# One PSUM bank for y and for the side work, a third bank for A dt, and side work that is begun only where it can end: a state-space layer with a feed-forward block on one NeuronCore

## The chip, the cores and the metric

The kernel runs on one core of a Trainium2 chip. The metric is the device time of one execution in microseconds. All arithmetic is in float32.

## The reference

Two layers follow each other on x of 2 sequences of 1024 tokens with 512 channels. The first is a selective state-space layer with N = 128 states per channel, the second a feed-forward block with 2048 hidden units. Each adds its result to its input and normalises it.

```python
xn = x * rsqrt(mean(x * x) + 1e-6) * norm_w
xn = xn * sigmoid((xn @ select_proj_w.T + select_proj_b) * select_gate)
delta, B, C = split(xn @ x_proj_w.T)                 # 128 columns each
delta = softplus(delta @ dt_proj_w.T + dt_proj_b)    # 512 channels
A = -exp(A_log)                                      # 512 x 128
for t in range(1024):
    h = exp(delta[t][:, None] * A) * h + (delta[t] * xn[t])[:, None] * B[t][None, :]
    y[t] = (h * C[t][None, :]).sum(-1)
x = layernorm(x + (y + x * D_param) @ out_proj_w.T)
x = layernorm(x + (silu(x @ w_gate.T) * (x @ w_up.T)) @ w_down.T)
```

## The kernel before

**Stages, halves and steps.** The 2048 tokens are cut into 64 stages of 32 tokens (`st`). A stage has two halves (`h = 2 * st + i`), and a half has eight steps (`r = k % 8`), so the main loop runs over `k` from 0 to 1023. A step covers 32 groups of channels for the 128 states: `[128 states, 32, 32 tokens]`, 1024 elements per partition.

**One step.** TensorE makes two matmuls of `bu` (dt x B, line 692) into one of two `bu` tiles of two PSUM banks each, and, between them, two matmuls of `a` (A dt, `decay_mm`, line 404) for the step after. Each `a` tile is one bank, from the pool `ps_a`, which has two. ScalarE takes the exponential of each `a` bank (`decay_exp`, line 411) into `a_sb`, which has three places. VectorE adds the state carried over from the stage before into the first token (line 705) and runs the scan `h = a * h + bu` along the tokens (line 708). GpSimd spreads dt and dt x over diagonal tiles (`diag`: `ddt`, line 375, and `du`, line 385), which the matmuls take as their moving operand.

**y.** `y_round(h, b)` is four 256-column matmuls that contract h with C for four tokens; a half needs eight rounds, and they read the half before. `ROUNDS` says at which of the eight steps they are issued: three after step 1, three after step 4, two after step 7. The two halves of a stage share one tile of the pool `ps_y`, a PSUM bank of its own. Once both are done, `y_out` (line 430) copies the bank to SBUF on ScalarE, and GpSimd picks the wanted elements and adds them up. Every fourth stage this adds a `post` generator: the transposes `zT`, the output projection `op`, the first norm.

**The side work.** All else is in generators that a small class, `Work`, advances between the steps: `pre` (the projections of the next lot of 256 tokens: `ss`, `sel`, `xp`, `b`, `z`, `uT`, `t0`), `post`, and `ffn` (`x1T`, gate and up `gu`, down `d`; its weights are streamed, four pieces of 512 KB ahead). A generator yields "E" where other engines' work follows, "P" where it wants to begin a run of matmuls in a PSUM bank, and "H" between the pieces of such a run. Only one run is under way at a time, since all of it uses a single bank (`ps_m`, tag "m", one buffer); the next run's first matmul waits until the last reader of the bank is done. `work.others()` runs at the start of each step and advances all generators that stand at "E". `work.tensor()` issues one piece after a step's matmuls. How many is set by `PARTS` and a running credit:

```python
credit = min(credit + PARTS[r], 6)
for _ in range(min(credit, 4) if PARTS[r] else 0):
    if not work.tensor():
        break
    credit -= 1
```

So a run may stand half done over a step that belongs to y. `work.finish` forces a lot's `pre` to its end before the stage that needs it. After the last scan the rest of the side work is run with six banks.

The order of the instructions of each engine is the order in which the program issues them. PSUM's eight banks are: two `bu` tiles (4), `a` (2), side work (1), y (1).

Of the kernel before, what the change touches and what calls it, by code (L numbers as in the profile page):

```python
# [9 lines left out]
FP = mybir.dt.float32  # L10
AF = mybir.ActivationFunctionType
ALU = mybir.AluOpType
# [3 lines left out]
P = 128  # L16
# [3 lines left out]

ROUNDS = ((), (0, 1, 2), (), (), (3, 4, 5), (), (), (6, 7))
PARTS = (4, 0, 3, 3, 0, 3, 3, 0)
RMS_EPS = 1e-6
# [11 lines left out]
def kernel(  # L35
# [17 lines left out]
    nc = tc.nc  # L53
# [67 lines left out]
    half_pool = tc.alloc_tile_pool(name="half", bufs=2)  # L121
    ps_y = tc.alloc_tile_pool(name="ps_y", bufs=1, space=PSUM)
    ps_m = tc.alloc_tile_pool(name="ps_m", bufs=1, space=PSUM)
# [34 lines left out]
    def misc(name):  # L158
        return bank_pool[0].tile([P, 512], FP, tag="m", name=name)
# [5 lines left out]
    def pre(c):  # L165
# [32 lines left out]
        for m in range(NM):  # L198
            nc.scalar.activation(xT[:, m, :], xT[:, m, :], AF.Copy, scale=col(V_NORM, m))
        yield "P"  # L200
        ps = misc(f"ss_{c}")
# [11 lines left out]
        for a in (slice(0, 2), slice(2, 4)):  # L213
# [3 lines left out]
            yield "E"  # L217
        yield "P"


        for m in range(NM):
            ps = misc(f"sel_{c}_{m}")
            yield from matmuls(ps, sel_w, m, xn)
            nc.scalar.activation(
                u[:, m, :], ps[:, 0:n], AF.Relu,
                bias=neg[:, 1, m : m + 1], scale=neg[:, 0, m : m + 1],
            )
            nc.scalar.activation(
                dt[:, m, :], ps[:, 0:n], AF.Abs, bias=gate_b[:, m : m + 1], scale=col(V_GATE, m)
            )  # L230
            yield "P" if m + 1 < NM else "E"
# [6 lines left out]
        yield "P"  # L238


        for g, dst in ((0, low), (2, c_sb)):
            ps = misc(f"xp_{c}_{g}")
            yield from matmuls(ps, xp_w, g, xn)
            nc.scalar.copy(dst, ps[:, 0:n])
            yield "P"

# [10 lines left out]
        for st in range(n_s):  # L257
# [4 lines left out]
            )  # L262
        yield "P"

        for a in range(0, NM, 2):
            ps = misc(f"z_{c}_{a}")
            for m in (a, a + 1):
                nc.tensor.matmul(  # L268
                    ps[:, ts(m - a, n)], dt_w[:, ts(m, P)], low, start=True, stop=True
                )  # L270
                yield "H" if m == a else "E"
            for m in (a, a + 1):
                z = ps[:, ts(m - a, n)]
                nc.scalar.activation(u[:, m, :], z, AF.Relu, bias=col(V_DTB, m))
                nc.scalar.activation(dt[:, m, :], z, AF.Abs, bias=col(V_DTB, m))
            yield "P" if a == 0 else "E"
        yield from softplus(dt, u)
# [4 lines left out]
        for j in range(n_j):  # L282
            yield "P"
            ps = misc(f"uT_{c}_{j}")
# [15 lines left out]
            if c == 0:  # L300
                load(0)
                diag(0, 0)
                diag(0, 1)
        yield "P"
        ps = misc(f"t0_{c}")
# [42 lines left out]
    def carry_a(st):  # L348

        if st % NSB == 0:  # L350
            return
        cd = carried[st]
        nc.gpsimd.tensor_tensor(cd, a_n, cd, ALU.mult)
        nc.scalar.activation(cd, cd, AF.Exp, scale=-1.0)

# [59 lines left out]
    def y_round(h, b):  # L415


        st, i = divmod(h, 2)
        if i == 0 and b == 0:
            ys[st] = ps_y.tile([P, 512], FP, tag="y", name=f"y_{st}")  # L420
        at = 28 + 28 * b
        for m in range(NM):
            nc.tensor.matmul(  # L423
                ys[st][ts(m, 32), ts(i, 256)], cz[st % 3][:, at : at + 32],
                hs[h][:, ts(m, 64), ts(b, 4)],
                start=(i == 0 and b == 0), stop=(i == 1 and b == 7),
                skip_group_check=True,
            )

    def y_out(st):  # L430

        tt, s = divmod(st, 4)
        if s == 0:
            yrs[tt] = post_pool.tile([P, 4, P], FP, tag="yr", name=f"yr_{tt}")
        yc = post_pool.tile([P, P, 4], FP, tag="yc", name=f"yc_{st}")
        nc.scalar.copy(yc, ys.pop(st).rearrange("p (q t) -> p q t", t=4))  # L436
        nc.gpsimd.tensor_tensor(yc, yc, pick.unsqueeze(1).to_broadcast([P, P, 4]), ALU.mult)  # L437
        nc.gpsimd.tensor_tensor(yc[:, :, 0:2], yc[:, :, 0:2], yc[:, :, 2:4], ALU.add)
        nc.gpsimd.tensor_tensor(yrs[tt][:, s, :], yc[:, :, 0], yc[:, :, 1], ALU.add)
        if s == 3:  # L440
            work.add(post(tt), front=True)
# [3 lines left out]
    def post(tt):  # L445
# [6 lines left out]
        yield "E"  # L452
        yield "P"
        ps = misc(f"zT_{tt}")
# [10 lines left out]
        nc.sync.dma_start(x1, xf[tt])  # L465
        yield "P"
        ps = misc(f"op_{tt}")
# [22 lines left out]
    def ffn(tt, row):  # L490
# [24 lines left out]
        x1T = ffn_pool.tile([P, NM, P], FP, tag="x1T", name=f"x1T_{tt}")  # L515
        yield "P"
        ps = misc(f"x1T_{tt}")
# [7 lines left out]
        for what in order:  # L525
            part = int(what[1])
            if what[0] == "g":
# [3 lines left out]
                for f in range(0, NH, 2):  # L531
                    fetch(at + 4)
                    yield "P"
                    ps = misc(f"gu_{tt}_{part}_{f}")
# [20 lines left out]
            for half in range(2):  # L555
                fetch(at + 4)
                yield "P"
                ps = misc(f"d_{tt}_{part}_{half}")
# [48 lines left out]
    class Work:  # L607


        def __init__(self):  # L610
            self.gens, self.holder = [], None

# [17 lines left out]

        def tensor(self):

            if self.holder is not None:
                if self.holder[1] != "H":
                    return False
                self.step(self.holder)
                return True
            for item in self.gens:
                if item[1] == "P":
                    self.holder = item  # L640
                    self.step(item)
                    return True
            return False

        def finish(self, item):
# [21 lines left out]
    pres, begun, credit = {}, set(), 0  # L667
    for k in range(NG):
        h, m, pair = place(k)
        st, i = divmod(h, 2)  # L670
        r = k % 8
        work.others()
        if r == 0:
            hs[h] = half_pool.tile([P, 256, S], FP, tag="h", name=f"h_{h}")

            if i == 1 and st:
                y_out(st - 1)
            if i == 0:
# [58 lines left out]
    y_out(NS - 1)  # L737
    ps_a.release()
# [8 lines left out]

    for pool in (bank_pool[0], ps_m, ps_y, hid_pool[0], ffn_pool, post_pool, main):
        pool.release()
# [67 lines left out]
```

## Time and profile before

| | |
|---|---|
| time, three runs | 2867.26, 2872.88, 2875.75 us (median 2872.88) |
| the profiled execution | 2875.05 us, span 2873.2 us |
| mean granted TensorE clock | 0.985 |
| TensorE matmuls busy | 2751.4 us, 96% |
| VectorE busy | 2532.2 us, 88%; of it the scans 1024 x 2.287 us |
| ScalarE busy | 1561.8 us, 54%; of it the exponentials of A dt 2048 x 0.585 us |
| GpSimd busy | 1783.0 us, 62% |
| first scan begins, last scan ends | at 42.5 us, at 2785.2 us |

The profile gives each group of instructions by the line of the kernel, the engine, and "out<-in" with the names of the tiles. In the timeline the first column is the start in microseconds from the span's start, the second the length, and brackets hold the idle time before it and what ended it. A float32 matmul shows as two rows, and rows overlap where matmuls run in different parts of the array or are still draining: so a matmul's cost is read from the start of one group to the start of the next.

### The profile page before, as it was taken

What the parts mean: (1) busy time and instruction counts of PE and PEld (TensorE: products, weight loads), DVE (VectorE), ACT (ScalarE), POOL (GpSimd) and SP (SyncE); (2) the same over time, 40 slices, a digit from 0 to 9 for tenths busy, and PEclk for the clock granted to TensorE, in tenths of its full rate; (3) what the DMA queues carried; (4) which work ended last, traced back from release to release, by engine and by line L of the source; (5) the groups of instructions that cost most, each with busy time, mean ns of one, the idle gap of its engine ahead of it and who ended that gap; (6) DMA issues with size and microseconds to landing.
All of it is one profiled execution on the core that took longest, in us unless ns stands there. A gap on an engine that the chain in (4) does not pass through costs nothing.

```text
span 2873.2 us, 57382 instructions
## 1 busy us (share of the span) xinstructions
PE 2751.4 (96%) x22728; PEld 1496.3 (52%) x22728; DVE 2532.2 (88%) x2176; ACT 1561.8 (54%) x3105; POOL 1783.0 (62%) x2016
## 2 busy tenths in 40 slices
PE   7879899999999999999999999999999999999998
PEld 4324455555555555455555555555555555555558
DVE  3999799899998999999999999999999999999970
ACT  4545555555565556645555555555556555555543
POOL 4556665666666666666567667566665666666643
PEclk6999999999999999999999999999999999999999
DMA  2011221324213231222312233122321322333236
GB/s 74 16 30 65 78 87 61 105 66 133 85 53 112 89 107 62 82 98 89 111 51 88 97 103 109 56 84 92 114 96 51 115 96 91 114 101 100 98 112 230
DMA packets 112379, 258.66 MB, mean 90 GB/s; under 512 B 11568, under 2 KB 49456, under 8 KB 112112
## 3 DMA queue, kind: packets, MB, share of 16 engines
q1 hardware_dynamic: 112112, 254.99, 27.4%
q8 instruction: 181, 2.97, 0.4%
q14 instruction: 86, 0.70, 0.1%
HBM read 242.23 MB, written 12.71 MB: 89 GB/s over the span
## 4 chain that ended last, share of the span: by engine, by line
PE 75%; DVE 18%; issue 3%; ACT 2%; POOL 1%; DMA 0%; SPq 0%; DVEq 0%; POOLq 0%; ACTq 0%
PE bu L692 27%; PE gu L539 17%; DVE h L708 16%; PE y L423 13%; PE d L561 6%; PE a L404 5%; PE sel L186 2%; PE op L470 1%; PE xp L186 1%; DVE bu L705 1%; ACT a_sb L411 1%; PE b L250 1%; PE ss L203 0%; PE z L268 0%; DMA ub_d<-uT 0%
## 5 line engine op out<-in xcount | busy, mean ns | idle before, releaser
L708 DVE TENSOR_TENSOR_SCAN h<-a_sb,bu 128x1024 f32<-128x1024 f32 x1024 | 2341.2, 2287 | 160.7 <-PE bu L692 46.3
L411 ACT ACTIVATE a_sb<-a 128x496 f32<-128x496 f32 x2048 | 1089.0, 585 | 1078.5 <-PE a L404 957.1
L404 PE MATMUL a<-ddt,a_t 32*128 32x512 f32 x4096 | 1253.9, 647 | 3.0 <-ACT t L314 2.8
L692 PE MATMUL bu<-du,ub 32*128 32x512 f32 x4096 | 1210.5, 647 | 47.9 <-DVE h L708 27.3
L375 POOL TENSOR_TENSOR ddt<-dt,hot 128x512 f32<-128x512 f32 x512 | 532.6, 1048 | 310.2 <-PE a L404 310.2
L539 PEld LDWEIGHTS gu<-x1T,w 128*128 128x128 f32 x4096 | 482.2, 192 | 230.9 <-issue 181.3
L385 POOL TENSOR_TENSOR du<-ub,hot 128x512 f32<-128x512 f32 x512 | 535.0, 1049 | 48.9 <-PE a L404 44.9
L539 PE MATMUL gu<-x1T,w 128*128 128x128 f32 x4096 | 537.1, 283 | 11.7 <-DVE x L474 4.0
L692 PEld LDWEIGHTS bu<-du,ub 32*128 32x128 f32 x4096 | 342.9, 185 | 376.9 <-issue 206.8
L423 PE MATMUL y<-h,cz 128*32 128x256 f32 x8192 | 527.3, 386 | 1.3 <-DVE h L708 1.3
L423 PEld LDWEIGHTS y<-h,cz 128*32 128x32 f32 x8192 | 228.2, 110 | 407.8 <-issue 296.4
L404 PEld LDWEIGHTS a<-ddt,a_t 32*128 32x128 f32 x4096 | 379.4, 185 | 31.3 <-ACT a_sb L411 19.9
L579 POOL TENSOR_SCALAR gu<-gu 128x256 f32<-128x256 f32 x128 | 108.3, 846 | 309.6 <-ACT gu L547 309.3
L705 DVE TENSOR_TENSOR bu<-bu,cd 128x32 f32<-128x32 f32 x992 | 185.6, 187 | 98.2 <-PE a L404 92.0
L561 PE MATMUL d<-w,hid 128*128 128x256 f32 x1024 | 256.7, 393 | 12.6 <-ACT t L314 4.4
L561 PEld LDWEIGHTS d<-w,hid 128*128 128x128 f32 x1024 | 183.9, 190 | 131.7 <-issue 86.1
L437 POOL TENSOR_TENSOR yc<-yc,pick 128x512 f32<-128x512 f32 x64 | 66.5, 1039 | 151.1 <-ACT yc L436 151.0
L362 POOL TENSOR_TENSOR cd<-cd,h 128x256 f32<-128x256 f32 x124 | 106.4, 858 | 45.5 <-DVE h L708 45.5
L587 POOL TENSOR_TENSOR hid<-gu,e 128x256 f32<-128x256 f32 x128 | 93.0, 727 | 62.1 <-ACT e L585 60.2
L547 ACT COPY gu<-gu 128x512 f32<-128x512 f32 x128 | 75.1, 587 | 63.2 <-PE gu L539 63.1
L580 POOL TENSOR_TENSOR gu<-gu 128x256 f32<-128x256 f32 x128 | 94.2, 736 | 10.7
L567 DVE TENSOR_TENSOR x<-x,d 128x256 f32<-128x256 f32 x64 | 25.6, 399 | 72.3 <-PE d L561 72.3
(86 smaller groups left out, 1272.1 us busy)
## 6 DMA issues: line engine op xcount, KB each, us to landing
w<-in_wgu_s_dram SPq DMA_DIRECT2D x256, 512.0 KB, 3.6
w<-in_wd_s_dram SPq DMA_DIRECT2D x128, 512.0 KB, 3.6
cd<-dt_d SPq DMA_DIRECT2D x62, 256.0 KB, 3.9
ub<-ub_d SPq DMA_DIRECT2D x64, 128.0 KB, 2.0
ub_d<-bt SPq DMA_DIRECT2D x64, 64.0 KB, 1.8
ub_d<-uT SPq DMA_DIRECT2D x64, 64.0 KB, 1.8
zT<-in_x_q_dram SPq DMA_DIRECT2D x16, 256.0 KB, 4.1
x<-in_x_dram SPq DMA_DIRECT2D x16, 256.0 KB, 3.8
```

The source lines that it names most:

```text
L362: nc.gpsimd.tensor_tensor(cd, cd, last, ALU.mult)
L375: nc.gpsimd.tensor_tensor(ddts[j][:, m, :, :], made[lot_of[st]][0][:, a + m, toks(st)].unsqueeze(1).to_broadcast([P, 16, S]), hot[:, ts(i, ...
L385: nc.gpsimd.tensor_tensor(dus[j][:, m, :, :], uv[:, a + m, :].unsqueeze(2).to_broadcast([P, 16, S]), hot.unsqueeze(1).to_broadcast([P, 16, ...
L404: nc.tensor.matmul(ps, a_t[ts(g, 32), m, :], ddts[k // 4][ts(g, 32), m % 2, :, :], start=True, stop=True,)
L411: nc.scalar.activation(a_sb[:, k % 3, ts(b, 16), 1:], ps[:, :, 1:], AF.Exp, scale=-1.0)
L423: nc.tensor.matmul(ys[st][ts(m, 32), ts(i, 256)], cz[st % 3][:, at : at + 32], hs[h][:, ts(m, 64), ts(b, 4)], start=(i == 0 and b == 0), s ...
L539: nc.tensor.matmul(ps[:, ts(2 * a + b, P)], w[:, a, k, :], x1T[:, k, :], start=(k == 0), stop=(k == NM - 1),)
L561: nc.tensor.matmul(ps[:, 0:HD], hid[:, f, :], w[:, f % 4, :], start=(f == 0), stop=(f == NH - 1),)
L579: nc.gpsimd.tensor_scalar_max(g, g, -80.0)
L692: nc.tensor.matmul(bu[:, ts(b, 16), :], prepared[st][ts(g, 32), 1, :], dus[k // 4][ts(g, 32), m % 2, :, :], start=True, stop=True,)
L705: nc.vector.tensor_tensor(first, first, left[:, at : at + 2, i, :], ALU.add)
L708: nc.vector.tensor_tensor_scan(hs[h][:, ts(r, 32), :].rearrange("p q t -> p (q t)"), a_sb[:, k % 3, :, :].rearrange("p q t -> p (q t)"), b ...
```

## The change

- The pool `ps_y` goes. y of a half (no longer of a stage) is a tile of the side work's bank, and `y_out` is called for each half, at the start of step 4.
- The eight rounds are issued in two runs of four, after steps 2 and 3. Ahead of the first, `work.idle()` ends whatever run of side work is open.
- The freed bank becomes a third buffer of `ps_a`.
- A generator yields the number of pieces of a run where it yielded "P", and `work.tensor(room)` begins a run only if that number fits into `ROOM` at this step. `PARTS` changes, and the credit is gone.
- The exponential of the carried decay is issued at the end of step 7, not with its product at step 5.

```diff
-ROUNDS = ((), (0, 1, 2), (), (), (3, 4, 5), (), (), (6, 7))
-PARTS = (4, 0, 3, 3, 0, 3, 3, 0)
+ROUNDS = ((), (), (0, 1, 2, 3), (4, 5, 6, 7), (), (), (), ())
+PARTS = (4, 4, 0, 0, 3, 3, 4, 4)
+
+ROOM = (8, 4, 0, 0, 8, 4, 4, 8)
...
-    ps_y = tc.alloc_tile_pool(name="ps_y", bufs=1, space=PSUM)
...
         nc.gpsimd.tensor_tensor(cd, a_n, cd, ALU.mult)
-        nc.scalar.activation(cd, cd, AF.Exp, scale=-1.0)
+
+    def carry_exp(st):
+        if st % NSB:
+            nc.scalar.activation(carried[st], carried[st], AF.Exp, scale=-1.0)
...
     def y_round(h, b):
...
-        st, i = divmod(h, 2)
-        if i == 0 and b == 0:
-            ys[st] = ps_y.tile([P, 512], FP, tag="y", name=f"y_{st}")
+        if b == 0:
+            ys[h] = misc(f"y_{h}")
...
-    def y_out(st):
-
+    def y_out(h):
+
+        st, i = divmod(h, 2)
...
-        yc = post_pool.tile([P, P, 4], FP, tag="yc", name=f"yc_{st}")
-        nc.scalar.copy(yc, ys.pop(st).rearrange("p (q t) -> p q t", t=4))
-        nc.gpsimd.tensor_tensor(yc, yc, pick.unsqueeze(1).to_broadcast([P, P, 4]), ALU.mult)
+        yc = post_pool.tile([P, 64, 4], FP, tag="yc", name=f"yc_{h}", bufs=2)
+        nc.scalar.copy(yc, ys.pop(h)[:, 0:256].rearrange("p (q t) -> p q t", t=4))
+        nc.gpsimd.tensor_tensor(yc, yc, pick.unsqueeze(1).to_broadcast([P, 64, 4]), ALU.mult)
...
-        def tensor(self):
+        def tensor(self, room=64):
 
             if self.holder is not None:
                 if self.holder[1] != "H":
                     return False
+                self.left -= 1
                 self.step(self.holder)
                 return True
             for item in self.gens:
-                if item[1] == "P":
-                    self.holder = item
+                if item[1] != "E" and item[1] <= room:
+                    self.holder, self.left = item, item[1] - 1
                     self.step(item)
                     return True
             return False
+
+        def idle(self):
+
+            while self.holder is not None:
+                self.others()
+                if self.holder is not None:
+                    self.tensor()
...
-    ps_a = tc.alloc_tile_pool(name="ps_a", bufs=2, space=PSUM)
+    ps_a = tc.alloc_tile_pool(name="ps_a", bufs=3, space=PSUM)
...
         work.others()
+        if r == 4 and h:
+            y_out(h - 1)
...
-        if h:
+        if ROUNDS[r] and h:
+            if r == 2:
+                work.idle()
             for b in ROUNDS[r]:
                 y_round(h - 1, b)
-        credit = min(credit + PARTS[r], 6)
-        for _ in range(min(credit, 4) if PARTS[r] else 0):
-            if not work.tensor():
-                break
-            credit -= 1
+        done = 0
+        while (done < PARTS[r] or done < 4 and work.left == 1) and work.tensor(ROOM[r] - done):
+            done += 1
...
+        if r == 7 and i == 0 and st + 1 < NS:
+            carry_exp(st + 1)
+    work.idle()
```

The numbers of pieces that replace "P" are: 4 for `ss`, `sel` and `xp`, 2 for `b` (1 in a lot of 128 tokens), `z`, `uT`, `zT` and `x1T`, 1 for `t0`, and 8 for `op`, `gu` and `d`. A piece is one matmul of `ss`, `sel`, `xp`, `z`, `op` or `d` (256 columns, in a full lot), two 128-column matmuls of `gu`, four of `b` or `t0`, or two transposes.

More of the change, by code (lines that the diff above doesn't have):

```diff
@@ L199, in pre @@
             nc.scalar.activation(xT[:, m, :], xT[:, m, :], AF.Copy, scale=col(V_NORM, m))
-        yield "P"
+        yield NM
         ps = misc(f"ss_{c}")
@@ L217, in pre @@
             yield "E"
-        yield "P"
+        yield NM
         for m in range(NM):
@@ L230, in pre @@
             )
-            yield "P" if m + 1 < NM else "E"
+            yield NM if m + 1 < NM else "E"
         yield from softplus(dt, u)
@@ L237, in pre @@
             yield "E"
-        yield "P"
+        yield NM
         for g, dst in ((0, low), (2, c_sb)):
@@ L244, in pre @@
             nc.scalar.copy(dst, ps[:, 0:n])
-            yield "P"
+            yield NM if g == 0 else n_j
         ps = misc(f"b_{c}")
@@ L262, in pre @@
             )
-        yield "P"
+        yield 2
         for a in range(0, NM, 2):
@@ L275, in pre @@
                 nc.scalar.activation(dt[:, m, :], z, AF.Abs, bias=col(V_DTB, m))
-            yield "P" if a == 0 else "E"
+            yield 2 if a == 0 else "E"
         yield from softplus(dt, u)
@@ L282, in pre @@
         for j in range(n_j):
-            yield "P"
+            yield 2
             ps = misc(f"uT_{c}_{j}")
@@ L303, in pre @@
                 diag(0, 1)
-        yield "P"
+        yield 1
         ps = misc(f"t0_{c}")
@@ L423, in y_round @@
             nc.tensor.matmul(
-                ys[st][ts(m, 32), ts(i, 256)], cz[st % 3][:, at : at + 32],
+                ys[h][ts(m, 32), 0:256], cz[h // 2 % 3][:, at : at + 32],
                 hs[h][:, ts(m, 64), ts(b, 4)],
-                start=(i == 0 and b == 0), stop=(i == 1 and b == 7),
+                start=(b == 0), stop=(b == 7),
                 skip_group_check=True,
             )
-    def y_out(st):
+    def y_out(h):
+        st, i = divmod(h, 2)
         tt, s = divmod(st, 4)
-        if s == 0:
+        if s == 0 and i == 0:
             yrs[tt] = post_pool.tile([P, 4, P], FP, tag="yr", name=f"yr_{tt}")
-        yc = post_pool.tile([P, P, 4], FP, tag="yc", name=f"yc_{st}")
-        nc.scalar.copy(yc, ys.pop(st).rearrange("p (q t) -> p q t", t=4))
-        nc.gpsimd.tensor_tensor(yc, yc, pick.unsqueeze(1).to_broadcast([P, P, 4]), ALU.mult)
+        yc = post_pool.tile([P, 64, 4], FP, tag="yc", name=f"yc_{h}", bufs=2)
+        nc.scalar.copy(yc, ys.pop(h)[:, 0:256].rearrange("p (q t) -> p q t", t=4))
+        nc.gpsimd.tensor_tensor(yc, yc, pick.unsqueeze(1).to_broadcast([P, 64, 4]), ALU.mult)
         nc.gpsimd.tensor_tensor(yc[:, :, 0:2], yc[:, :, 0:2], yc[:, :, 2:4], ALU.add)
-        nc.gpsimd.tensor_tensor(yrs[tt][:, s, :], yc[:, :, 0], yc[:, :, 1], ALU.add)
-        if s == 3:
+        nc.gpsimd.tensor_tensor(yrs[tt][:, s, ts(i, 64)], yc[:, :, 0], yc[:, :, 1], ALU.add)
+        if s == 3 and i == 1:
             work.add(post(tt), front=True)
@@ L452, in post @@
         yield "E"
-        yield "P"
+        yield 2
         ps = misc(f"zT_{tt}")
@@ L465, in post @@
         nc.sync.dma_start(x1, xf[tt])
-        yield "P"
+        yield 2 * NM
         ps = misc(f"op_{tt}")
@@ L515, in ffn @@
         x1T = ffn_pool.tile([P, NM, P], FP, tag="x1T", name=f"x1T_{tt}")
-        yield "P"
+        yield 2
         ps = misc(f"x1T_{tt}")
@@ L532, in ffn @@
                     fetch(at + 4)
-                    yield "P"
+                    yield 2 * NM
                     ps = misc(f"gu_{tt}_{part}_{f}")
@@ L556, in ffn @@
                 fetch(at + 4)
-                yield "P"
+                yield NH
                 ps = misc(f"d_{tt}_{part}_{half}")
@@ L610, in __init__ @@
         def __init__(self):
-            self.gens, self.holder = [], None
+            self.gens, self.holder, self.left = [], None, 0
         def add(self, gen, front=False):
@@ L662 @@
     ps_bu = tc.alloc_tile_pool(name="ps_bu", bufs=2, space=PSUM)
-    ps_a = tc.alloc_tile_pool(name="ps_a", bufs=2, space=PSUM)
+    ps_a = tc.alloc_tile_pool(name="ps_a", bufs=3, space=PSUM)
     for b in range(2):
         decay_exp(0, b, decay_mm(0, b))
-    pres, begun, credit = {}, set(), 0
+    pres, begun = {}, set()
     for k in range(NG):
@@ L672 @@
         work.others()
+        if r == 4 and h:
+            y_out(h - 1)
         if r == 0:
             hs[h] = half_pool.tile([P, 256, S], FP, tag="h", name=f"h_{h}")
-            if i == 1 and st:
-                y_out(st - 1)
             if i == 0:
@@ L734 @@
             carry_a(st + 1)
+        if r == 7 and i == 0 and st + 1 < NS:
+            carry_exp(st + 1)
+    work.idle()
     for j in range(8):
         y_round(2 * NS - 1, j)
-    y_out(NS - 1)
+    y_out(2 * NS - 1)
     ps_a.release()
@@ L746 @@
         work.tensor()
-    for pool in (bank_pool[0], ps_m, ps_y, hid_pool[0], ffn_pool, post_pool, main):
+    for pool in (bank_pool[0], ps_m, hid_pool[0], ffn_pool, post_pool, main):
         pool.release()
```

## The prediction

> **What bounds the kernel now.** I read the page first (busy shares, then the chain that ended last), then TensorE's timeline in the middle of the run, then its waits and the end of the run.
>
> ```profile
> PE 2751.4 (96%) x22728; PEld 1496.3 (52%) x22728; DVE 2532.2 (88%) x2176; ACT 1561.8 (54%) x3105; POOL 1783.0 (62%) x2016
> PE 75%; DVE 18%; issue 3%; ACT 2%; POOL 1%; DMA 0%; SPq 0%; DVEq 0%; POOLq 0%; ACTq 0%
> ```
>
> TensorE and VectorE are both nearly full, and the chain runs three quarters on TensorE. A busy TensorE is not one that only works, so its steps have to be priced. The timeline of TensorE (start, length, then what runs) gives the prices:
>
> ```profile
> 1400.46 0.69 PE L692 MATMUL bu<-du,ub 32*128 32x512 f32 x1
> 1400.46 0.69 PE L404 MATMUL a<-ddt,a_t 32*128 32x512 f32 x1
> 1400.47 0.69 PE L692 MATMUL bu<-du,ub 32*128 32x512 f32 x1
> 1400.83 0.69 PE L404 MATMUL a<-ddt,a_t 32*128 32x512 f32 x1
> ...
> 1401.88 1.50 PE L423 MATMUL y<-h,cz 128*32 128x256 f32 x24
> 1403.32 0.69 PE L692 MATMUL bu<-du,ub 32*128 32x512 f32 x1
> ...
> 1404.39 2.05 PE L539 MATMUL gu<-x1T,w 128*128 128x128 f32 x16
> 1406.37 0.69 PE L692 MATMUL bu<-du,ub 32*128 32x512 f32 x1
> ```
>
> Read start to start. The four matmuls of one step run side by side: 1403.32 to 1404.39 is 1.07 us. In the step at 1400.46 the second A dt matmul comes 0.37 us late, because its bank was not yet read, and the step takes 1.42. Three rounds of y take 1.44 and two take 1.00 (at 1418.66), so 0.43 a round and 0.14 for each run. Sixteen rows (8 matmuls) of gate/up take 1.98, twelve 1.54: 0.22 a matmul and 0.20 for each run of side work; a 256-column matmul is 0.43. VectorE repeats every 2.48 us where it doesn't wait (its timeline at 1400.48, 1402.96, 1405.44), so 19.87 a half of 8 steps. The halves of before average 21.3 us (start to start of every eighth scan), and TensorE's priced work in them about 20.2: TensorE sets the pace, and what it loses is waits. From its start times: of 989 steps between 100 and 2750 us, 236 have a late second A dt matmul, and they are longer by 120 us together. Idle time ahead of side work, after 360 us, is 32 us.
>
> **The change part by part**, with counts from the changed kernel's order of instructions.
>
> (1) TensorE's work in the loop. 127 fewer runs of y (two a half, not three): -17.5. Side work is in 618 runs, not 589: +5.7. Sixteen down matmuls and 64 gate/up move from the end into the loop: 6.9 + 14.3. So +9 in all. But where it lies counts: a half lasts at least the greater of its TensorE work and 19.87. Summed over 127 halves that is 2577 before and 2609 after: **+32**. The new order repeats every 16 halves and is uneven: one holds 16.8 us (VectorE sets it) and the next 23.8.
>
> (2) Third bank. An exp starts 0.13 us after a step's matmuls end (1430.81 to 1430.94), takes 0.58, and its bank is used 0.06 later. With two banks a following step less than about 1.2 us away waits; with three, the second A dt matmul needs only the first exp, 0.77 after the step's end. That still costs 0.77 where two steps follow each other with nothing between. ROOM = 4 at step 1 keeps an 8-piece gate/up out, and step 1 is empty of side work in 76 halves, just ahead of step 2: 58 us. So -120 + 58 = **-62**. None of it saved if the waits have another cause; nothing left of the 58 if TensorE is ahead and waits for h there anyway: -120 to 0.
>
> (3) The one shared bank. A piece read by VectorE isn't free until the add has had its turn, and that add stands behind the scan of the step in which the piece ended. From a step's end: 0.18 to the small add, 0.30 to the scan, 2.20 until the next instruction, 0.40 for the add of d, 0.06: 3.1 us. The trace has such waits:
>
> ```profile
> 356.93 1.99 PE L561 MATMUL d<-w,hid 128*128 128x256 f32 x8 [0.50 <-DVE x L567]
> 1112.50 3.37 PE L470 MATMUL op<-out_w,zT 128*128 128x256 f32 x8 [1.21 <-DVE zT L461]
> 341.20 1.59 PE L307 MATMUL t<-ident,dt 128*8 128x128 f32 x8 [3.14 <-ACT uT L291]
> 345.09 1.22 PE L561 MATMUL d<-w,hid 128*128 128x256 f32 x2 [2.29 <-ACT t L314]
> ```
>
> The first: 6 rows of d (1.49) and a step (1.07) cover 2.56 of 3.1; 0.57 by the sum, 0.50 by the row. In the new order d ends at step 6 on two matmuls (1.06) and the next piece begins at step 7, 30 times: 3.1 - 2.13 = 1.0 each, 30 us. zT ends at step 7 and op begins at step 0, 15 times: the zT add is 0.66, so 3.4 - 0.59 - 1.07 = 1.74, 26 us. uT, uT, t0 now fall at steps 7, 0, 1 with y at 2, all in that bank, 7 times. Each copy on ScalarE waits for the DMAs that read the row tile before it (3.2 us after the last copy, from 337.37 to 340.56), with the exps queued behind it: t0 finds the bank 2.1 late and y 1.9, and uT 0.2: 29 us. op ahead of y (15 x 0.4), z ahead of gate/up (6 x 1.0) and the rest: 17. Together 102 against the 32 of before: **+70**. From below: about +20, if half of it falls where VectorE sets the pace; from above +100, if the row's DMAs take 5 us (as at 1558 to 1564) and not 3.2.
>
> (4) Lead. No row shows it: the empty step 1 gives TensorE 1.41 us at once, and it can't be far ahead of the two bu banks. Between 0 and 54 us (half that slack in 76 halves); I take **+20**, nearer the lower end, because in most halves VectorE is already waiting by then.
>
> (5) Clock. The windows view of before has stretches at half clock (start:end, then busy times; the ninth column is the granted clock):
>
> ```profile
> 1109.50:1112.90 3.40, 2.19 (x11) 1.15 (x11) 3.22 (x4) 1.99 (x5) 3.00 (x4) 1.00 0.00 0
> 1112.90:1116.30 3.40, 3.40 (x12) 2.30 (x14) 2.05 (x1) 0.00 (x0) 1.56 (x3) 0.51 0.00 0
> ```
>
> A wait of 1.21 us behind transposes was followed by 3.4 us at half clock: op took 3.37, not 1.92. With the step after it that is about 1.7 lost; it happened three times after 360 us, among eleven waits of 0.8 us and more that followed transposes. The Trainium skill, page "TensorE: Matmul & The Clock Gate", section "Part 1: The HAM clock gate", asks for a whole idle window of about 3.4 us before the clock falls. By the rule the new waits of 1 to 2 us cost nothing here; by the row, some 36 such waits give about ten falls, 17 us against 5: **+12**. I go by the row.
>
> (6) The end and the first lots. After the last scan (2785.17) before still has half a feed-forward layer, then a whole one, 88.0 us. After, only 8 down matmuls of the former are left. The pieces: d 1.9 past the scan, its add and y to 6.0, copy and picking 2.1, zT and its add 1.6, op 3.6, norm 3.5 now uncovered, x1T 2.7, then the 50.4 that before has from 2822.80: about 70. **-18**. The forced end of a lot's side work at 335 us (VectorE waits 10.7 us there) is gone, since uT and t0 end earlier: **-11**.
>
> Costed at nothing: 64 copies of y at 0.585 become 128 of about 0.37 (a 128x256 PSUM copy's row), and picking 64 x 2.07 on GpSimd becomes 128 x about 1.5. ScalarE's 957 us of waits for A dt and GpSimd's 310 for a free ddt hide them; uncovered it would be 10 and 60. The y copy stands ahead of two exps, but the step's matmuls (1.07) run meanwhile; du and ddt behind picking are needed three steps later. The cd exp goes behind the exps of step 7; its 15.3 us of waiting for GpSimd ends, already in (2). Scans reuse h after y: y now ends at step 3, not 7, so nothing waits. SP's queue keeps four weight pieces ahead (3.6 us to land).
>
> The sum: 32 - 62 + 70 + 20 + 12 - 18 - 11 = +43 on a span of 2873.2, so 2916. The profiled run's time (2875.05) is 1.85 above its span and 2.2 above the median; the median should be 2916 too.
>
> **The rivals.**
> A, faster: step 2 does not wait behind the empty step 1. Then (2) is -120 and (4) falls to 0, so 43 - 58 - 20 = -35: 2838. It decides once steps 1 to 2 lose less than 0.2 us of the 0.77 together with the lead lost. For it: nothing in before shows three banks, and VectorE's floor of 19.87 a half would allow it. Against: TensorE's own work in these halves is 20.4, so it arrives late and finds the exp pending.
> B, slower still: the chain of row tile, bank and y. If each DMA takes 5 us, 7 x 4 more, and every such wait brings the half clock, 29 more: 2970.
> C, it cancels: the shared bank's waits fall into VectorE-bound halves (+20 instead of +70) and the gain of the third bank stands: 43 - 50 = -7, 2866 to 2881. That is the change doing nothing that can be told.
>
> **How the numbers follow.** The forecast, 2890 to 2945, has 0.65; B 0.15; C 0.08; A 0.12. The range 2866 to 2962 leaves out A and the top of B. No change means within 0.3% (2864 to 2881), about what a measurement of this kernel can tell. Faster 0.12, same 0.08, slower 0.80.
>
> **What would show it.** In the profile after: y in two runs of 32 rows at 1.87 us; late second A dt matmuls only at step 2; waits of op for the zT add near 1.7 us, about 15 times, of d for the x add near 1.0, and of y for the copy of t0; halves of about 22 us where d follows d; half-clock stretches behind zT; about 70 us past the last scan. It is wrong if VectorE's steps fall below 2.6 us on average, or if TensorE's waits for VectorE's adds stay under 30 us.

## The result, and the profile after

The changed kernel takes 2960.72 us (median of four runs, 2955.73 to 2962.16), the kernel before 2872.28 (2867.26 to 2875.75): a ratio of 1.0306, 95% interval [1.0287, 1.0326], 88 us slower. The direction was forecast, and the time lies just inside the range (2866 to 2962), but the change is twice the 43 us of the sum.

The page of the changed kernel, busy times and the chain that ended last:

```profile
PE 2753.4 (93%) x22728; PEld 1472.2 (50%) x22728; DVE 2554.5 (86%) x2176; ACT 1577.4 (53%) x3169; POOL 1817.5 (61%) x2208
PE 78%; DVE 13%; issue 4%; ACT 2%; POOL 1%; DMA 1%; SPq 0%; DVEq 0%; ACTq 0%; POOLq 0%
```

TensorE is busy as long as before in a span 87 us longer, and VectorE's share of the chain fell from 18% to 13%: the pace is still TensorE's, and what was added is waiting and slower work. Its waits (line waited, releaser, us in total, times, longest):

```profile
PE bu L704 <- DVE bu L717: 59.1, 64, 1.4
PE op L474 <- DVE zT L465: 25.3, 16, 1.8
PE d L565 <- DVE x L571: 21.6, 23, 1.2
PE uT L287 <- ACT uT L292: 13.4, 7, 1.9
PE t L308 <- ACT uT L292: 8.6, 7, 1.9
...
PE y L426 <- ACT t L315: 5.3, 4, 1.7
```

All rows of this view for side work and y together (everything but `bu` and `a`) are 127.9 us, against 64.0 before. VectorE's own view shows the other side of it: its waits for a step's matmuls, which the view puts down to the A dt ones among them, are 167.1 us (266 times, longest 3.2), against 92.0 (174 times, longest 10.7).

The span and the mean granted clock, first of before, then of the changed kernel:

```profile
core 0: 2873.2 us, clock 0.985
```

```profile
core 0: 2960.4 us, clock 0.965
```

(1 - clock) x span is the clock that TensorE didn't get: 43 us before, 104 us after. From the 112th step (at about 350 us) to the last scan, the clock records of the trace hold 3 stretches at half clock before, 10.2 us together, and 20 after, 105.8 us. By the last wait ahead of its start, 6 of the 20 (37.6 us) follow a wait of `uT`, 4 (13.7 us) a wait of `op`, and 10 (54.6 us) follow steps without side work, in which only `bu` waited for VectorE. Two of these in the windows view of the changed kernel, each with the stretch ahead of it and the one behind it (busy us and count of TensorE, its weight loads, VectorE, ScalarE, GpSimd, then the granted clock):

```profile
1217.20:1224.00 6.80, 4.76 (x40) 2.61 (x40) 6.45 (x7) 5.41 (x11) 6.72 (x8) 1.00 0.11 45
1224.04:1230.87 6.83, 5.56 (x24) 1.64 (x21) 3.44 (x3) 2.56 (x6) 4.06 (x5) 0.50 0.32 77
1230.87:1237.70 6.83, 6.83 (x92) 3.41 (x89) 5.60 (x6) 3.29 (x7) 2.28 (x4) 1.00 0.27 82
1329.90:1336.60 6.70, 4.24 (x32) 1.69 (x31) 6.39 (x6) 5.14 (x11) 5.01 (x7) 1.00 0.39 105
1336.68:1343.50 6.82, 6.00 (x44) 2.34 (x48) 5.43 (x5) 1.63 (x4) 3.25 (x4) 0.50 0.46 185
1343.50:1350.30 6.80, 6.80 (x64) 3.13 (x61) 5.13 (x6) 2.86 (x6) 3.35 (x6) 1.00 0.00 0
```

What TensorE did just ahead of and in these stretches (start, length, then in brackets the wait before it), first around 1224, then the three empty steps ahead of 1337 and the first run of y behind them:

```profile
1223.26 0.66 PE L287 MATMUL uT<-ident,u 128*128 128x128 f32 x4 [1.94 <-ACT uT L292]
1227.07 1.88 PE L308 MATMUL t<-ident,dt 128*8 128x128 f32 x8 [1.27 <-ACT uT L292]
1230.92 1.94 PE L426 MATMUL y<-h,cz 128*32 128x256 f32 x32
1233.86 1.94 PE L426 MATMUL y<-h,cz 128*32 128x256 f32 x32
...
1332.64 0.66 PE L704 MATMUL bu<-du,ub 32*128 32x512 f32 x1 [0.79 <-DVE bu L717]
...
1335.02 0.66 PE L704 MATMUL bu<-du,ub 32*128 32x512 f32 x1 [1.23 <-DVE bu L717]
...
1337.50 1.19 PE L704 MATMUL bu<-du,ub 32*128 32x512 f32 x1 [1.34 <-DVE bu L717]
...
1339.52 3.64 PE L426 MATMUL y<-h,cz 128*32 128x256 f32 x32
```

and VectorE behind that run:

```profile
1344.53 0.20 DVE L717 TENSOR_TENSOR bu<-bu,cd 128x32 f32<-128x32 f32 x1 [2.21 <-PE a L408]
```

ScalarE's copies of the two uT:

```profile
1222.64 0.57 ACT L292 COPY uT<-uT 128x512 f32<-128x512 f32 x1
1226.43 0.59 ACT L292 COPY uT<-uT 128x512 f32<-128x512 f32 x1 [1.96 <-DMA ub_d<-uT]
```

At 1223 the second uT waits 1.94 us for the shared bank, since the copy of the first stands behind other work in ScalarE's queue; at 1227 t0 waits 1.27 us for the second copy, which waited for the DMAs of the row tile. 6.8 us at half clock begin between the two. At 1337 nothing was late: three steps in a row had no side work, so TensorE waited 0.79, 1.23 and 1.34 us for VectorE. The run of y behind them took 3.64 us and not 1.94, and now VectorE waited 2.21 us for TensorE.

The end of the kernel, from the last scan on:

```profile
2887.57 2.29 DVE L720 TENSOR_TENSOR_SCAN h<-a_sb,bu 128x1024 f32<-128x1024 f32 x1
2891.17 0.42 DVE L571 TENSOR_TENSOR x<-x,d 128x256 f32<-128x256 f32 x1 [1.31 <-PE d L565]
```

The last scan ends at 2889.86, 70.5 us before the span ends. Before it was 88.0. The loop from the 112th step to the last scan takes 2538 us, not 2436, and what lies ahead of it 352, not 349.

### The profile page after: what moved, and what is told of

Same layout as the page of the kernel before. It is cut to its first block, busy times and chain, and to the rows that moved or that the text cites. A ratio compares the mean times of both kernels' runs of the same rounds, so it can differ in the third digit from the quotient of the medians.

```text
span 2960.4 us, 58093 instructions
## 1 busy us (share of the span) xinstructions
PE 2753.4 (93%) x22728; PEld 1472.2 (50%) x22728; DVE 2554.5 (86%) x2176; ACT 1577.4 (53%) x3169; POOL 1817.5 (61%) x2208
## 4 chain that ended last, share of the span: by engine, by line
PE 78%; DVE 13%; issue 4%; ACT 2%; POOL 1%; DMA 1%; SPq 0%; DVEq 0%; ACTq 0%; POOLq 0%
PE bu L704 29%; PE gu L543 17%; PE y L426 16%; DVE h L720 11%; PE d L565 7%; PE a L408 4%; PE sel L187 2%; PE op L474 1%; PE xp L187 1%; DVE bu L717 1%; ACT a_sb L415 1%; DMA ub_d<-uT 1%; PE b L251 1%; PE ss L204 1%; DVE x L571 0%
## 5 line engine op out<-in xcount | busy, mean ns | idle before, releaser
L704 PE MATMUL bu<-du,ub 32*128 32x512 f32 x4096 | 1196.3, 661 | 67.4 <-DVE bu L717 59.1
L704 PEld LDWEIGHTS bu<-du,ub 32*128 32x128 f32 x4096 | 330.5, 188 | 427.1 <-issue 241.5
L426 PE MATMUL y<-h,cz 128*32 128x256 f32 x8192 | 510.6, 391 | 10.9 <-ACT t L315 5.3
L426 PEld LDWEIGHTS y<-h,cz 128*32 128x32 f32 x8192 | 243.7, 111 | 360.6 <-issue 181.8
L408 PEld LDWEIGHTS a<-ddt,a_t 32*128 32x128 f32 x4096 | 351.6, 188 | 47.6 <-ACT a_sb L415 43.6
L717 DVE TENSOR_TENSOR bu<-bu,cd 128x32 f32<-128x32 f32 x992 | 188.5, 190 | 180.7 <-PE a L408 167.1
L441 POOL TENSOR_TENSOR yc<-yc,pick 128x256 f32<-128x256 f32 x128 | 78.5, 613 | 389.2 <-ACT yc L440 389.1
L366 POOL TENSOR_TENSOR cd<-cd,h 128x256 f32<-128x256 f32 x124 | 106.3, 858 | 80.8 <-DVE h L720 75.1
L584 POOL TENSOR_TENSOR gu<-gu 128x256 f32<-128x256 f32 x128 | 93.2, 728 | 10.7
L440 ACT COPY yc<-y 128x256 f32<-128x256 f32 x128 | 47.6, 372 | 94.4 <-PE y L426 93.6
L474 PE MATMUL op<-out_w,zT 128*128 128x256 f32 x256 | 72.6, 434 | 25.3 <-DVE zT L465 25.3
```

What stands on the lines that cost most here:

```text
L366: nc.gpsimd.tensor_tensor(cd, cd, last, ALU.mult)
L408: nc.tensor.matmul(ps, a_t[ts(g, 32), m, :], ddts[k // 4][ts(g, 32), m % 2, :, :], start=True, stop=True,)
L426: nc.tensor.matmul(ys[h][ts(m, 32), 0:256], cz[h // 2 % 3][:, at : at + 32], hs[h][:, ts(m, 64), ts(b, 4)], start=(b == 0), stop=(b == 7), ...
L704: nc.tensor.matmul(bu[:, ts(b, 16), :], prepared[st][ts(g, 32), 1, :], dus[k // 4][ts(g, 32), m % 2, :, :], start=True, stop=True,)
L717: nc.vector.tensor_tensor(first, first, left[:, at : at + 2, i, :], ALU.add)
```

## Experiments

Times are medians in us; each ratio is to the kernel before on the same chip. "Before" was 2872 to 2875 in all of them. Code cuts leave lines out; "..." stands between separate places.

### A ladder from before to the change, one part at a time

**y of a half, all else as before.** The order, rounds, places and credit of before; `y_out` once a half at step 0, the carried decay's exp at the end of step 7.

```diff
-            ys[st] = ps_y.tile([P, 512], FP, tag="y", name=f"y_{st}")
+            ys[h] = ps_y.tile([P, 512], FP, tag="y", name=f"y_{h}")
...
+        if r == 0 and h > 1:
+            y_out(h - 2)
```

> Before with two of the change's parts alone: y is a tile of a half (its own bank, as before, read at step 0 after its last round) and the carried decay's exp comes at the end of step 7. The rounds (3, 3, 2), the pieces per step, the credit and the freedom to begin a run anywhere are those of before. Theory (these two are covered): 64 more copies of 0.37 us on ScalarE and 64 more picks on GpSimd lie beside TensorE's work: 2866 to 2882, no change. Rival (the halves themselves cost part of the order's +103 us): the copy at step 0 makes the first round of y, at step 1, or two exps late in each half; 0.3 us a half would be 38 us: 2900 and more.

2867.44, ratio 0.9979 [0.9969, 0.9989]. As the theory has it: the 64 further copies and picks are covered.

**y bunched.** Banks, credit and freedom to begin a run are those of the last one. With the rounds, the places of the side work move too (`PARTS`), and `y_out` comes at step 4.

```diff
-ROUNDS = ((), (0, 1, 2), (), (), (3, 4, 5), (), (), (6, 7))
-PARTS = (4, 0, 3, 3, 0, 3, 3, 0)
+ROUNDS = ((), (), (0, 1, 2, 3), (4, 5, 6, 7), (), (), (), ())
+PARTS = (3, 3, 0, 0, 3, 3, 2, 2)
```

> The version with before's order and y of a half in its own bank (2867), with y alone bunched: four rounds after steps 2 and 3, read at step 4, as in the change. Side work keeps the credit of 16 pieces a half and may begin anywhere; its places are 3, 3, 0, 0, 3, 3, 2, 2. Counted from the order of instructions with the durations of the trace of before, the sum over the steps of the greater of TensorE's work and VectorE's 2.48 rises by 35 us in 904 steps, some 40 in all, and about 20 us less is left for the end. Theory (placing of side work makes most of the order's 103 us, bunching little): 2875 to 2900. Rival (two steps of 2.94 us in a row make it, since TensorE has no lead to take them from): 2940 to 2976.

2931.52, ratio 1.0195 [1.0178, 1.0211]: 62 us more than the one before it, between theory and rival and the largest single part of the loss. (The run doesn't part the bunching from the new places that it forces.) TensorE's waits for side work and y rose from 57.6 to 96.8 us. The rows that grew, first with the rounds spread:

```profile
PE d L566 <- DVE x L572: 4.4, 8, 1.2
...
PE gu L544 <- ACT x1T L528: 3.6, 4, 2.1
PE t L309 <- ACT uT L293: 3.2, 1, 3.2
```

and with y bunched:

```profile
PE t L309 <- ACT uT L293: 13.8, 7, 3.2
...
PE gu L544 <- ACT x1T L528: 7.8, 7, 1.4
PE d L566 <- DVE x L572: 7.2, 10, 1.3
PE gu L544 <- ACT t L316: 7.1, 5, 2.9
```

y has its own bank in both kernels, so nothing of this is the sharing. With y spread, a step of y stands between the runs of side work about every third step, and while it runs, the reader of the one side bank finishes. With y in two steps, the other six in a row are left to side work, and a run meets the bank of the run just ahead. In the timeline with y bunched:

```profile
1585.52 0.65 PE L288 MATMUL uT<-ident,u 128*128 128x128 f32 x4 [0.20 <-ACT uT L293]
1589.33 1.04 PE L309 MATMUL t<-ident,dt 128*8 128x128 f32 x8 [1.73 <-ACT uT L293]
1594.32 3.39 PE L544 MATMUL gu<-x1T,w 128*128 128x128 f32 x16 [2.88 <-ACT t L316]
```

The gate/up behind t0 is 2.88 us late and then runs at a clock of 0.57 (windows view, 1594.32 to 1597.72): 3.39 us for a run that took 2.05 in the kernel before.

**The change's rule and places, y in its own bank, two A dt banks.** This is the change without its two bank moves.

```diff
+    ps_y = tc.alloc_tile_pool(name="ps_y", bufs=1, space=PSUM)
...
-            ys[h] = misc(f"y_{h}")
+            ys[h] = ps_y.tile([P, 512], FP, tag="y", name=f"y_{h}")
...
-    ps_a = tc.alloc_tile_pool(name="ps_a", bufs=3, space=PSUM)
+    ps_a = tc.alloc_tile_pool(name="ps_a", bufs=2, space=PSUM)
```

> As the run with two A dt banks, but y has a bank of its own again (y of a half, same order, still preceded by the end of the open run). My theory: only y's own waits for the bank go (15 x 0.4 behind op, 7 x 1.9 behind t0, 19 us) and some half clock behind t0, so 20 to 35 us less than the run with two A dt banks. Rival (sharing the bank is the chief cost of the change): 60 us less or more, back to the time of the kernel before.

2975.78, ratio 1.0357 [1.0337, 1.0376]: 47 us over the last one. The order alone therefore costs over 100 us before any bank is moved.

**The same with y in the shared bank, the eighth bank idle.**

```diff
-    ps_a = tc.alloc_tile_pool(name="ps_a", bufs=3, space=PSUM)
+    ps_a = tc.alloc_tile_pool(name="ps_a", bufs=2, space=PSUM)
```

> The changed kernel with the third bank of A dt taken away again (two banks, the eighth bank unused); the order of all instructions is the same. My theory: the third bank is worth its late-matmul waits, 45 to 60 us, so this takes 3005 to 3020 us against 2961 for the changed kernel, and late second A dt matmuls come back at several steps. Rival: the added time is all in waits of the shared bank and TensorE would have waited anyway; then this stays within 9 us of 2961.

3006.95, ratio 1.0467 [1.0445, 1.0488]. So sharing the bank costs 1.10% (31 us), and the third A dt bank, which separates this kernel from the change, gives 46 us back; both as the theories had it. The ladder in per cent of before: -0.21 (halves), +2.16 (bunching y), +1.62 (rule and places), +1.10 (sharing), -1.61 (third bank): +3.06. Each interval is about 0.2 to either side.

The profiled executions show what goes with each rung (us). "Late A dt" is counted from the start times: by how much the second A dt matmul of a step starts after the step's first matmul, summed over the steps after 100 us where it is more than 0.12.

| kernel | span | loop from the 112th step | after the last scan | waits for side work and y | late A dt | clock not granted |
|---|---|---|---|---|---|---|
| before | 2873.2 | 2436 | 88 | 64 | 104 | 43 |
| y of a half | 2873.4 | 2437 | 88 | 58 | 106 | 49 |
| y bunched | 2924.9 | 2501 | 66 | 97 | 95 | 73 |
| rule and places | 2967.9 | 2545 | 68 | 105 | 152 | 68 |
| y in the shared bank | 2999.5 | 2572 | 68 | 119 | 152 | 87 |
| the change | 2960.4 | 2538 | 71 | 128 | 46 | 104 |

Bunching brings waits and lost clock. Rule and places bring little of either, but lateness: at step 2, behind the step 1 that `ROOM` leaves empty, it grows from 22 to 95 us. The third bank takes 105 us of lateness away and gives 46 us of time, so lateness counts for less than its size, and the columns are no sum.

### What the waits for the side bank cost

**Two side banks** in place of the third A dt bank.

```diff
-    ps_m = tc.alloc_tile_pool(name="ps_m", bufs=1, space=PSUM)
+    ps_m = tc.alloc_tile_pool(name="ps_m", bufs=2, space=PSUM)
...
-    ps_a = tc.alloc_tile_pool(name="ps_a", bufs=3, space=PSUM)
+    ps_a = tc.alloc_tile_pool(name="ps_a", bufs=2, space=PSUM)
```

> As the run with two A dt banks, but the side work and y have two banks in turn. My theory: the waits for the reader of the last piece go (d at step 7: 30 us, t0 and y behind the row copies: 28, z and op: 12, and half clock behind them), 60 to 80 us less than the run with two A dt banks; the wait of op for the zT add stays, since it is for data. Rival (the loss is the uneven filling of the steps, not the bank): under 25 us less.

2962.65, ratio 1.0312 [1.0289, 1.0336]: 44 us under the version with one side bank, between the rival's 25 and the 60 to 80 expected. The waits for side work fell from 119.1 to 50.4 us, but the half clock did not (75.1 and 85.3 us from the 112th step on). One row stayed, in the view of this kernel:

```profile
PE op L474 <- DVE zT L465: 25.5, 16, 1.8
```

A second bank doesn't touch it: op waits for the zT that VectorE's add writes, its own input, and not for the bank.

**Two row tiles.** The row tile is the SBUF tile that uT and t0 are copied into, and that DMAs then read.

```diff
-            t = pre_pool.tile([P, D], FP, tag="row", name=f"uT_{c}_{j}")
+            t = pre_pool.tile([P, D], FP, tag="row", bufs=2, name=f"uT_{c}_{j}")
```

> The changed kernel with two buffers for the row tile that uT and t0 copy into. My theory: the copies no longer wait for the DMAs of the row before, so the chain uT, uT, t0, y loses its 4 us in each of seven lots (29 us), and with it the half-clock stretches of 6.8 us that begin in the sixth half of each lot (about 3 us each, 20 in all): 2912 to 2930 us against 2961. Rival (the half clock comes from steps without side work, not from these waits): only the 29 us or less go, 2932 to 2945, and the stretches stay.

2929.44, ratio 1.0198 [1.0182, 1.0214]: 31 us less for seven places in the run, as the theory had it. The wait of t0 (8.6 us) left the list, uT's (13.4) stayed, since the two uT follow each other in one bank. All waits for side work and y fell by 15 us (127.9 to 112.5), and the clock not granted by about 20 (104 and 84, means of the four runs of each). The stretches at half clock behind uT's wait are still there, but the five of them last 3.4 us and not 6.8.

**d's and zT's banks read by ScalarE**, their adds on GpSimd from SBUF. The lines for d; those for zT are alike.

```diff
-                nc.vector.tensor_tensor(part_of, part_of, ps[:, 0:HD], ALU.add)
+                nc.scalar.copy(dc, ps[:, 0:HD])
+                nc.gpsimd.tensor_tensor(part_of, part_of, dc, ALU.add)
```

> The changed kernel, but the banks of d and of zT are copied out by ScalarE and added by GpSimd, so that no read of them stands behind a scan in VectorE's queue. My theory: d's wait at step 7 goes (30 pieces x 1.0 us), op's wait for zT shortens from 1.7 to about 1.2 us (15 x 0.5), and part of the half clock behind it goes: 2910 to 2925 us against 2961. Rival: the copies queue behind the exps and GpSimd's adds come late, so the waits only change their name; within 15 us of 2961.

2949.27, ratio 1.026 [1.0241, 1.028]: 12 us, a third of what the theory had and inside the rival's 15. d's wait went; op's grew:

```profile
PE op L476 <- POOL zT L467: 35.3, 16, 3.8
```

The add of zT that op waits for takes 1.26 us on GpSimd (0.66 on VectorE); six of the 16 begin only 0.9 to 1.3 us after the copy, behind GpSimd's own work, and nine waited for ScalarE's copy. So for half of the edit the wait only changes its name, as the rival had it.

### The clock

**Filler matmuls** in the version with the eighth bank idle: two 256-column matmuls without a reader in every step that has neither y nor side work.

```diff
+        if not done and not (ROUNDS[r] and h):
+            fill = ps_f.tile([P, 512], FP, tag="f", name=f"f_{k}")
+            for b in range(2):
+                nc.tensor.matmul(
+                    fill[:, ts(b, 256)], sel_w[:, b, 0:P], out_w[:, b, 0:256], start=True, stop=True
+                )
```

> The run with two A dt banks, with two 256-column matmuls more (1.06 us with their start) in every step that has neither side work nor y, into the eighth bank, which nobody reads. It does work that no result needs. My theory: TensorE waits in those steps anyway (for A dt, h or the row), and the half-clock stretches that begin there (75 us of half clock after the first lots) mostly go: 2970 to 2985 us against 3007. Rival: the half clock costs nothing, since it falls where TensorE waits; then it stays at 3007 or rises.

2974.22, ratio 1.0341 [1.0323, 1.0359]: 33 us faster by doing more. The core lines without and with the filler:

```profile
core 0: 2999.5 us, clock 0.971
```

```profile
core 0: 2973.0 us, clock 0.986
```

The waits for side work are the same (119.1 and 116.6 us). The filler went into 151 steps. Between these two executions (3001.26 and 2974.85 us) the clock not granted fell from 87 to 42 us: 26 us of time for 45. Over the means of the four runs of each it is 34 us for 61 (98 and 37). So a microsecond of clock not granted is worth 0.55 to 0.6 us of time here, an estimate; the filler's own time is in it.

### Where the side work is put

**No rule**: the version with y's own bank, its runs begun anywhere.

```diff
-            if r == 2:
-                work.idle()
...
-        while (done < PARTS[r] or done < 4 and work.left == 1) and work.tensor(ROOM[r] - done):
+        while (done < PARTS[r] or done < 4 and work.left == 1) and work.tensor():
```

> The version with y's own bank and two A dt banks (2976), without the rule: a run of side work may begin at any step, may stand half done across the y steps, and nothing is ended ahead of y. y stays in two runs of four rounds at steps 2 and 3. Theory (the rule makes the loss: it leaves step 1 empty ahead of two full steps and leaves pieces for late): the uneven halves even out, most of the +103 us of the order goes: 2885 to 2920, and the half-clock stretches fall below 8. Rival (the two bunched runs of y make it: steps 2 and 3 take about 2.9 us each whatever fills step 1): 2945 to 2975.

3086.07, ratio 1.0734 [1.0715, 1.0753]. Both theories missed: without the rule it is 110 us slower. The places of the change allow 22 pieces a half (before's credit allows 16), and it was the rule that held them back. Freed of it, the work is done in bursts and then missing: the mean clock is 0.954, and the stretches at half clock come to 187.7 us from the 112th step on, up to 17.1 us at a time.

**Other places**: at most 3 pieces at steps 6 and 7, runs of 8 allowed at 5 to 7; first in the change, then with y's own bank and two A dt banks.

```diff
-PARTS = (4, 4, 0, 0, 3, 3, 4, 4)
-ROOM = (8, 4, 0, 0, 8, 4, 4, 8)
+PARTS = (4, 4, 0, 0, 3, 3, 3, 3)
+ROOM = (8, 4, 0, 0, 8, 8, 8, 8)
```

> The change with other places for the side work alone: at most 3 pieces at steps 6 and 7 (not 4), and a run of 8 may begin at steps 5, 6 and 7 too (only 4 before). Rules, banks, y and the row tile stay. It spreads a run of 8 over three steps, so that fewer steps stand empty. Theory (empty steps cost what TensorE loses in lead and clock): the version with this, two row tiles and ScalarE's reading took 2884; less the 31 us and 12 us that those two brought alone, this is worth about 34 us: 2920 to 2932. Rival (the three help each other, since a spread run ends later and its reader then stands in the next run's way): 2940 to 2960.

2959.77, ratio 1.029 [1.0272, 1.0308]: nothing (1.0306 before the edit), as the rival had it. Under it two things move and cancel: late A dt falls from 46 to 23 us and the clock not granted from 104 to 74, but the waits for side work and y rise from 127.9 to 164.2.

> The change's rule with y in its own bank and two A dt banks (2976), with other places alone: at most 3 pieces at steps 6 and 7, and a run of 8 may begin at steps 5, 6 and 7 too. By the order of instructions 42 steps stand empty between the 112th and the 1016th, not 107, and 379 hold more than 2.9 us of TensorE's work, not 460; the sum of the greater of TensorE's work and 2.48 falls by 35 us, some 40 in all. Theory (a step's own work counts, not a half's): 2932 to 2945. Rival (a half's sum counts, which this change raises by 9 us): 2970 to 2990.

2981.09, ratio 1.0367 [1.035, 1.0385], against 1.0357: nothing either, inside the rival's range. Here late A dt falls from 152 to 121 us, and the clock not granted rises from 68 to 92. Fewer empty steps (42 and not 107) and fewer full ones don't pay by themselves, so a step-by-step count of TensorE's work doesn't price this order. Of the 47 us that rule and places make in the ladder, the 57 us of lateness that they add would be about 25 at the rate of the third bank (46 for 105), an estimate that no run tests; the rest stays open.

**Other places with both readings and two row tiles**, in the change, then the same with zT's bank left to VectorE.

> The changed kernel with two row tiles, the reads of d and zT on ScalarE and GpSimd, and other places: three pieces at steps 6 and 7, and a run of 8 pieces may begin at any of steps 4 to 7. My theory: the row tile gives its 31 us, the reads some 40, and the places 20 to 30 (fewer empty steps, so fewer late A dt matmuls and less half clock): 2850 to 2870 us against 2961, under the kernel before if the third bank's 46 us stand. Rival: the three overlap (each removes the same half-clock stretches), and 2890 or more is left.

2884.02, ratio 1.0033 [1.002, 1.0045]: better than the change by 77 us, between the theory's 2870 and the rival's 2890.

> The change with the other places (2960), two row tiles, and d's bank alone copied by ScalarE and added by GpSimd; zT's bank stays with VectorE. With zT's moved as well it took 2884. Theory (on GpSimd zT's add makes op wait longer, 20 us over 10 waits there): 2872 to 2882. Rival (it is zT's reader, behind VectorE's scan, that keeps the shared bank from y and the next run): 2888 to 2905.

2884.77, ratio 1.0032 [1.0019, 1.0046], between theory and rival. The same: with these places it doesn't matter who reads zT.

### The two edits outside the change

**In the kernel before**, two row tiles and ScalarE's reading, of both banks and then of d's alone.

> The kernel before, with d and zT read by ScalarE and added by GpSimd, and two row tiles. My theory: its own few waits behind the scan (about 20 us) and behind the row DMAs (about 10) go, some of it only to come back as waits for A dt: 2840 to 2855 us against 2873. Rival: the kernel before is bound by the A dt banks alone, and nothing is gained: 2865 or more.

2848.20, ratio 0.9905 [0.989, 0.992], as the theory had it.

> Before with two row tiles and the bank of d copied by ScalarE and added by GpSimd; zT's bank is read by VectorE as in before. The version that also moved zT took 2848. Theory (zT's reading on GpSimd made op wait longer, as in the changed kernel, 35 us against 25): without it 2838 to 2846. Rival (in the order of before zT's reader is not what ends a wait, VectorE gains by doing less): 2848 to 2856.

2846.02, ratio 0.9897 [0.9882, 0.9913]. The two can't be told apart; both beat the kernel before by about 1%, and this is the fastest version found.

**With y bunched**, y and side work in banks of their own.

> The version with y alone bunched, with two row tiles and d's bank copied by ScalarE and added by GpSimd. The two took 29 us off the kernel before (2846). Theory: the same here, 25 to 35 below the version with y bunched; it beats 2846 only if that one is under 2876. Rival (bunched y hides these waits already): 10 or less.

2885.18, ratio 1.0028 [1.0016, 1.004]: 46 us under the bunched version, more than the theory's 35 and the 29 that they give in the order of before. Its waits for side work fell by 38 us, from 96.8 to 59.2; in the order of before the same edits took 14 (64.0 to 49.8). So at least the 17 us between the two gains are bunching that uncovers the readers of the side bank and of the row tile. The other 45 us of bunching's 62 are not settled by this run; the clock not granted is 24 us more with y bunched (0.975 of 2924.9 us, against 0.983 of 2873.4), and 35 more in the means of all runs (78 and 43), which is part of them.

## Why the prediction was off in size

**(5) The clock is the step that failed.** It counted falls behind transposes only, one in four of such waits, ten in all, and took +12. Ten did come behind waits of `uT` and `op`, but 6.8 us long in five of the six behind `uT`, where 3.4 was taken. Ten more, over half of the time at half clock, began behind steps without side work (1337 above), which the new order has and which the prediction put at nothing. One of the three falls in the trace of before had already followed no transpose but a matmul of d:

```profile
1307.50 1.86 PE L539 MATMUL gu<-x1T,w 128*128 128x128 f32 x7 [1.20 <-DVE x L567]
```

The clock not granted rose by 61 us (48 of them from the 112th step to the last scan, half of the 105.8 less half of the 10.2); at the filler's rate that is about 35 us of time, an estimate, and not 12. Going by the row and not by the page's rule was right, and the count was still far too low. That leaves about 20 of the missing 45 us. What (2) and (6) below had too favourable is large enough for them, but it overlaps with the clock, and no run parts it.

**(2) The third bank** did what was counted, and it was worth less. Late A dt fell from 104 to 46 us (120 to 58 forecast). Of 238 late second matmuls 104 are left, 72 of them at step 2, behind an empty step 1. But in the order of the change the bank takes away 105 us of lateness for 46 us of time: the prediction took each microsecond of it as one of time. What the bank would give in the order of before, no run shows.

**(3) The shared bank**: the size of the waits was right, the cause half wrong. Waits for side work and y rose by 64 us (70 forecast): op 16 times 1.58 us (15 times 1.74), d 23 times 0.94 (30 times 1.0), and in the row tile's chain uT 1.9, t0 1.2 and y 0.8 us a lot (0.2, 2.1 and 1.9), 27 us in all for 29: near by luck, since the longest wait is the one that it put at 0.2, for a copy that is late in ScalarE's own queue. But sharing y's bank makes 31 us of the time; with y in its own bank these waits are already at 104.6. The prediction had the rows and put them down to the wrong part: to the sharing, where most of them come with the bunching already (57.6 to 96.8), which leaves runs of side work back to back. And op's wait is no bank wait.

**(1) and (4), unevenness and lead**, +52 together, were not measured apart. Bunching, rule and places make 62 + 47 = 109 us together; these two terms, 47 us of waits (57.6 to 104.6), lateness, the clock and (6) are all in it, and how much is (1) or (4) stays open.

**(6)** The end was right (70.5 us, "about 70"). The forced end of a lot is gone (VectorE's longest wait for A dt in the loop is 3.2, not 10.7), but its 11 us did not come: the part ahead of the 112th step takes 352 us, 3 more than before, with 44 us of clock not granted in it and not 36. So of the 45 us missing from the sum 30 are in the loop (+102, where the terms of the loop gave +72) and 14 ahead of it. What was costed at nothing (copies and picks of halves, the cd exp) costs nothing: 2867 in the first rung.

**The rivals.** A (2838) is out: step 2 does wait, and the order costs more than the bank gives. C (cancels) is out as well. B had the direction of the miss: the chain of row tile and bank does bring half clock (the six stretches behind `uT`), and two row tiles give 31 us, though the waits fall by only 15. Its slow DMAs are not the chief part: the longest wait of the chain, uT's, stays with two row tiles.

## What to carry over

A bank that is freed by moving two users together has to be paid for with the order that the sharing forces: price the order first, with the bank moves left out. Work of a second kind between two runs in one bank is the cover of that bank's reader; before bunching it, ask what will stand between the runs. Where TensorE is the bound, count the empty stretches of its queue as well as its waits, since both were followed here by several us at half clock. And a step left empty just ahead of another makes the next one's A dt late when its banks are few.

## What was not expected of the hardware

The half clock came after far less idleness than the rule that the prediction weighed (the Trainium skill, "TensorE: Matmul & The Clock Gate", "Part 1: The HAM clock gate": a whole idle window of about 3.4 us). In the 6.7 us ahead of 1336.68 TensorE was busy for 4.24 us and its longest whole wait was 1.23. The stretches come in lengths of 3.4 or 6.8 us, and up to 17.1 us where the side work ran out; in the changed kernel all 20 begin on one grid of 3.41 us. Of the pieces of that grid at full clock, from the 112th step to the last scan, 21 have TensorE busy for less than half: 17 of them were followed by half clock, and of the 692 others 3. It is no sharp rule: the three falls before followed pieces that were busy for 60 to 68%. And 33 us were gained by matmuls whose results nobody reads.
